# Token sums between the MLP's additions, and the first frequencies loaded between two halves of the row transforms

## The chip, the cores and the metric

The kernel runs on one core of one Trainium2 chip. The metric is device time in microseconds (us). Before the change, three runs gave a median of 3037.29 us, from 3034.9 to 3040.88. TensorE (PE) multiplies and transposes, VectorE (DVE) and ScalarE (ACT) empty PSUM and do elementwise work, GpSimd (POOL) does elementwise work in SBUF, and SyncE (SP) issues all the DMAs.

## The reference

The input is one image of 48 x 48 tokens with 768 channels, in float32. Two layers follow each other.

The first is a transformer block: layer norm, attention with 12 heads and relative positions over rows and columns, a projection, a residual, a second layer norm and an MLP:

```python
x = shortcut + out
xn2 = layernorm(x, ln2_g, ln2_b)
h = jax.nn.gelu(xn2 @ mlp_w1 + mlp_b1, approximate=False)      # 768 -> 3072
return x + (h @ mlp_w2 + mlp_b2)                               # 3072 -> 768
```

The second is a mixing in the frequencies of the image, with 8 blocks of 96 channels:

```python
xf = jnp.fft.rfft2(x, axes=(1, 2), norm='ortho')               # rows, then columns
o1 = relu(complex block product of xf with w1, plus b1)
o2 = softshrink(complex block product of o1 with w2, plus b2)
y = jnp.fft.irfft2(o2, s=(H, W), axes=(1, 2), norm='ortho')    # columns, then rows
return y + x
```

(The two middle lines stand for the four real products in the reference.)

## The kernel before, in words

Up to the MLP nothing changes: queries, keys and values, attention and the projection come first. The tokens, with the residual added, lie in SBUF as `x1`, 18 tiles of 128 tokens by 768 channels.

**The MLP** (lines 893 to 1068) takes the tokens in three passes `p` of 768. Each product of matrices is done in seven block products instead of eight, from sums and differences of blocks. For this, `xt` holds a pass's normalised tokens with channels on the partitions, in four blocks (lower and upper channels, first and second 384 tokens), and `xs` holds three sums of them. `sums_of_tokens` (line 163) makes these with four VectorE subtractions of 128 x 1152 numbers; they appear in the profile as L158, L159, L160 and L161. The last of the four overwrites one of the blocks of `xt`.

In a pass, `hidden` makes 256 of the 3072 hidden units, and there are twelve such steps. Between its three parts the additions `added(p, n - 1, i)` (line 975) of the step before are set, for `i` of 0 to 2. Each is seven products of 128 x 384 in four PSUM banks `o0` to `o3`, and VectorE adds each product to `x1` or to a sum `acc`, straight from PSUM (L995, L1001). So TensorE can be ahead of VectorE by about as many products as there are banks. In steps 4 to 9 of passes 0 and 1, `normalised` makes the normalised tokens (`hat2`, six buffers) for the next pass.

After the twelfth step comes the border: `turned` transposes the next pass's tokens on TensorE, ACT and VectorE write them to `xt` (L1045, L1049), `sums_of_tokens` is called, the three last additions of the old pass follow, and then `rows_forward(p)`. That multiplies the finished tokens with the Fourier matrix of the rows, first for the lower 384 channels (`k` of 0), then for the upper (`k` of 1). Each half has eight tiles in each pass: matmuls to `zp` in the same four banks, a copy to `zt` (four buffers; VectorE and ACT take turns, L77 and L75), and a store to the DRAM tensor `z1[k]` (L1026). The next pass's `hidden` comes after that.

**The spectral part** (lines 1070 to 1258) reads `z1` back in 14 units, seven for each half of the channels, of four frequencies each (the seventh has one). A unit is loaded as one tile `zi` (L1130, three buffers) and goes through four stages, one a round: `columns` (Fourier over columns, `fp`), `first` and `second` (the two block products, `lp` and `mp2`), and `back` (inverse over columns, `yp`; stored to `z2` at L1215). In one round four units are at work, each in another stage. `rows_back` is a generator for a group of 384 tokens and one half of the channels: a load of `zo` (L1222), then three steps of row transform (`rps`), addition of `x1`, and store. From round 11 on, its steps for the first half of the channels are set one by one between the stages; those of the second half follow at the end.

**What sets the order.** In the MLP and in the spectral part only TensorE's order is that of the program (`manual_schedule`). On the other engines and on SP's queue of DMAs, a planner chooses when the program is built: it goes by the order of the program, its own costs and what its costs say is ready. An engine and SP's queue then run in the order chosen, and an instruction that waits holds all behind it. A tile waits for the last use of the memory that it lies on. The pools of a closed part of the program give their memory to the next part, so such waits also run between parts.

Of the kernel before, what the change touches and what calls it, by code (L numbers as in the profile page):

```python
# [9 lines left out]
F32 = mybir.dt.float32  # L10
# [3 lines left out]
ALU = mybir.AluOpType  # L14
# [4 lines left out]
P = 128  # L19
HW = 48  # L20
T = HW * HW
NT = T // P
C = 768
# [6 lines left out]
G = 384  # L30
NB = 8
BS = C // NB
CH = C // 2
KW = HW // 2 + 1
# [10 lines left out]
def block_then_afno(  # L45
# [25 lines left out]
    nc = tc.nc  # L71
# [22 lines left out]
    z1 = [dram.tile([HW * 2 * KW, CH], F32, name=f"z1_{k}") for k in range(2)]  # L94
# [14 lines left out]
    xt = shared[:, : NC * TB].rearrange("p (c t) -> p c t", c=NC)  # L109
    xs = shared[:, NC * TB :].rearrange("p (k c t) -> p k c t", k=3, c=3)  # L110
# [46 lines left out]
    def right(eng, b11, b12, b21, b22, t):  # L157
        eng.tensor_tensor(t[0], b12, b11, ALU.subtract)  # L158
        eng.tensor_tensor(t[1], b22, t[0], ALU.subtract)  # L159
        eng.tensor_tensor(t[2], b21, t[1], ALU.subtract)  # L160
        eng.tensor_tensor(b12, b22, b12, ALU.subtract)  # L161

    def sums_of_tokens(xt, xs):
        lo, hi = xt[:, 0:3], xt[:, 3:6]
        right(
            nc.vector, lo[:, :, :G], lo[:, :, G:], hi[:, :, :G], hi[:, :, G:],
            [xs[:, i] for i in range(3)],
        )

    def parts_of_tokens(xt, xs, at=slice(None)):  # L170

# [13 lines left out]
    with ExitStack() as flag_scope:  # L185
# [11 lines left out]
        with ExitStack() as att:  # L197
# [314 lines left out]
            with tc.manual_schedule(engines={mybir.EngineType.PE, mybir.EngineType.SP}):  # L512
# [70 lines left out]
                for n, (pr, c, u) in enumerate(runs):  # L583
# [9 lines left out]
                    for i in range(RUN):  # L593
                        kt = RUN * u + i
                        p = exps[:, (RUN * n + i) % 18]
# [7 lines left out]
                    if pr < NC - 1:  # L603
                        if (c, u) in ((3, 1), (4, 0), (4, 1)):
                            i = 2 * (2 * (c - 3) + u - 1)
# [55 lines left out]
        with tc.tile_pool(name="ps_flag", bufs=1, space=PSUM) as psum, tc.tile_pool(  # L661
            name="ps_early", bufs=2, space=PSUM
# [29 lines left out]
        with tc.If(safe < 1):  # L692
            with ExitStack() as att:
                xnT = main.rearrange("p (c t) -> p c t", c=NC)
                with tc.tile_pool(name="g_ln1", bufs=3) as ln1, tc.tile_pool(
                    name="g_ps_ln1", bufs=2, space=PSUM
                ) as psum:
                    for g in range(T // G):
                        hats = []
# [179 lines left out]
        with tc.tile_pool(name="ps_proj", bufs=2, space=PSUM) as psum:  # L879
            hats = []  # L880
            for t in range(EARLY, NT):
# [8 lines left out]
                if n == 5:  # L890
                    sums_of_tokens(xt, xs)

    with ExitStack() as mlp:
        bias = mlp.enter_context(tc.tile_pool(name="mlp_const", bufs=1))
        b2 = bias.tile([P, C], F32, name="b2")
# [79 lines left out]
        def added(p, n, i):  # L975

            h, hs, v, vs = kept[p, n]
            bank = [psum.tile([P, CH], F32, name=f"o{k}") for k in range(4)]
            if n == 0:
                acc[i] = upool.tile([P, CH], F32, name=f"acc{i}", bufs=1)  # L980
            a11, a12, s3, a22 = (
                h[:, f, ds(k * G + i * P, P)] for f, k in ((0, 0), (1, 0), (0, 1), (1, 1))
            )
            s1, s2, s4 = (hs[:, k, ts(i, P)] for k in range(3))
            b11, t3, b21, b22 = (v[:, f, ts(k, CH)] for f in range(2) for k in range(2))
            t1, t2, t4 = (vs[:, k] for k in range(3))
            t = 2 * (p * 3) + i
            x11, x12, x21, x22 = (
                x1[:, t + 3 * j, ts(k, CH)] for j in range(2) for k in range(2)
            )  # L990

            def product(k, a, b, start, *into):
                nc.tensor.matmul(bank[k], a, b, start=start, stop=True, skip_group_check=not start)  # L993
                for dst in into:
                    nc.vector.tensor_tensor(dst, bank[k], dst, ALU.add)  # L995

            nc.tensor.matmul(bank[0], a11, b11, start=True, stop=True)  # L997
            if n == 0:
                nc.vector.tensor_copy(acc[i], bank[0])
            else:  # L1000
                nc.vector.tensor_tensor(acc[i], bank[0], acc[i], ALU.add)  # L1001
            product(1, s2, t2, True, acc[i])
            product(2, s3, t3, True, x22)
            product(3, s1, t1, True, x22)
            product(0, a12, b21, False, x11)
            product(2, a22, t4, False, x21)
            product(3, s4, b22, False, x12)
            if n == n_f - 1:
                nc.vector.tensor_tensor(x21, x21, acc[i], ALU.add)
                nc.gpsimd.tensor_tensor(x12, x12, acc[i], ALU.add)  # L1010
                nc.gpsimd.tensor_tensor(x22, x22, acc[i], ALU.add)

        def rows_forward(p):

            for k in range(2):
                for g in (2 * p, 2 * p + 1):
                    for a, parts in enumerate(((0,), (1, 2), (3, 4), (5,))):
                        zp = psum.tile([2 * 2 * KW, CH], F32, name="zp", tag=f"o{a}")
                        for b in parts:
                            nc.tensor.matmul(  # L1020
                                zp, rows_dft[:, b, :], x1[:, 3 * g + b // 2, ts(k, CH)],
                                start=(b == parts[0]), stop=(b == parts[-1]),
                            )
                        zt = upool.tile([2 * 2 * KW, CH], F32, name="zt", bufs=4)
                        balanced_copy(a, zt, zp)
                        nc.sync.dma_start(out=z1[k][ts(4 * g + a, 4 * KW), :], in_=zt)  # L1026

        hats = {}

        def normalised(p, i):  # L1030

            t = 6 * p + i
            hats[i] = hpool.tile([P, C], F32, name="hat2", bufs=6)
            normalise(upool, x1[:, t, :], hats[i])
            nc.gpsimd.tensor_tensor(x1[:, t, :], x1[:, t, :], b2, ALU.add)

        def turned():
            for j in range(2):
                for c in range(NC):
                    tp = psum.tile([P, G], F32, name="tp2", tag=f"h{c % 4}")  # L1040
                    for i in range(3):
                        nc.tensor.transpose(tp[:, ts(i, P)], hats[3 * j + i][:, ts(c, P)], ident)
                    dst = xt[:, c, ts(j, G)]
                    if c % 2:
                        nc.scalar.activation(  # L1045
                            dst, tp, AF.Identity, bias=col(V_LN2B + c), scale=col(V_LN2G + c)
                        )
                    else:
                        nc.vector.tensor_scalar(  # L1049
                            dst, tp, col(V_LN2G + c), col(V_LN2B + c), ALU.mult, ALU.add  # L1050
                        )
            sums_of_tokens(xt, xs)

        with tc.manual_schedule(engines={mybir.EngineType.PE}):
            for p in range(T // TB):
                for n in range(n_f):
                    work = hidden(p, n)
                    for i in range(3):
                        next(work)
                        if n:  # L1060
                            added(p, n - 1, i)
                    if p < 2 and 4 <= n < 10:
                        normalised(p + 1, n - 4)
                if p < 2:
                    turned()
                for i in range(3):
                    added(p, n_f - 1, i)
                rows_forward(p)

    with ExitStack() as sp:  # L1070
# [39 lines left out]
        nc.vector.tensor_scalar(a2i[:, :, 0, :], a2[:, :, 1, :], -1.0, None, ALU.mult)  # L1110
        nc.vector.tensor_copy(a2i[:, :, 1, :], a2[:, :, 0, :])

        z1_h = [z.rearrange("(r k) c -> r k c", k=KW) for z in z1]
        z2_h = [z.rearrange("(h t k) c -> h t k c", t=2, k=KW) for z in z2]
        NBH = NB // 2

        class Unit:
# [8 lines left out]
                self.zz = []  # L1126

            def load(self):
                self.zi = zin.tile([2 * HW, 4, CH], F32, name="zi", bufs=3)
                nc.sync.dma_start(  # L1130
                    out=self.zi[:, : self.nk, :],
                    in_=z1_h[self.half][:, self.k0 : self.k0 + self.nk, :],
                )

            def columns(self, i):

                if i == 0:
                    self.xf = mid.tile([BS, NBH, 2, 4, HW], F32, name="xf")
                if i >= self.nk:
                    return  # L1140
                fp = psum.tile([BS, NBH, 2, HW], F32, name="fp", tag="f")
                for b in range(NBH):
                    nc.tensor.matmul(  # L1143
                        fp[:, b].rearrange("p t h -> p (t h)"), self.zi[:, i, ts(b, BS)], cols,
                        start=True, stop=True,
                    )
                balanced_copy(i, self.xf[:, :, :, i, :], fp)
# [96 lines left out]
        with tc.manual_schedule(engines={mybir.EngineType.PE}):  # L1244
            first_half = pieces(ends[0])
            for r in range(len(units) + 3):
                if r < len(units):
                    units[r].load()
                for i in range(4):
                    for stage, lag in (("back", 3), ("second", 2), ("first", 1), ("columns", 0)):  # L1250
                        if 0 <= r - lag < len(units):
                            getattr(units[r - lag], stage)(i)
                    if r > len(units) // 2 + 3:
                        next(first_half, None)
            for _ in first_half:
                pass
            for _ in pieces(ends[1]):
                pass
# [128 lines left out]
```

## Time and profile before

| | us |
|---|---|
| median of three runs (lowest, highest) | 3037.29 (3034.9, 3040.88) |
| the profiled execution, its own time | 3041.24 |
| its span, from first to last instruction | 3039.4 |
| TensorE busy | 2947.5 |
| VectorE busy | 1784.6 |
| ScalarE busy | 869.5 |
| GpSimd busy | 569.2 |
| mean granted clock of TensorE | 0.99 |

In the profile a group of lines is named by its source line and engine, with the tile written, the tiles read, the shape and the count. A matmul in float32 is two instructions. A wait is put down to what ended it. The MLP lasts from about 1661 us to 2726 us of the span, with borders between the passes at about 1975 and 2335 us; the spectral part follows up to the end.

### The profile page before, as it was taken

To read this page: it belongs to the slowest core of one execution; us is meant where nothing else is said; L and a number is where in the kernel's file an instruction comes from. 1 tells how busy PE (TensorE), PEld (TensorE's weight loads), DVE (VectorE), ACT (ScalarE), POOL (GpSimd) and SP (SyncE) were. 2 spreads that over 40 slices of the span, in tenths; PEclk is the share of its full clock that TensorE was granted. 3 is DMA by queue.
4 is the path that set the end of the run, shared out by engine and by line. 5 is a ranking of instruction groups with operands and counts; after the bars stand their busy time and mean duration, and the time that the engine had idled before them with its cause. 6 is when DMAs were issued, how large, how long until landed. Compare 5 with 4: busy or idle time off the path is not lost. (4 is left out here: it accounts for less than half of the span.)

```text
span 3039.4 us, 40414 instructions
## 1 busy us (share of the span) xinstructions
PE 2947.5 (97%) x15495; PEld 1783.8 (59%) x15495; DVE 1784.6 (59%) x2582; ACT 869.5 (29%) x1346; POOL 569.2 (19%) x510
## 2 busy tenths in 40 slices
PE   6999999999999999999999999989999999989998
PEld 3555655655555565555555555555555555548885
DVE  4332327777777777777624766666666566653443
ACT  1010126565556565565401111121111111101110
POOL 2302110000000000000233332243223222211210
PEclk9999999999999999999999999999999999999999
DMA  3423276172552616344331111121111211131324
GB/s 110 144 80 115 97 158 123 29 134 56 87 114 50 135 32 132 64 81 74 130 116 46 52 63 63 52 64 63 62 53 52 74 62 52 52 94 55 90 70 151
DMA packets 204144, 253.37 MB, mean 83 GB/s; under 512 B 21698, under 2 KB 185762, under 8 KB 202406
## 3 DMA queue, kind: packets, MB, share of 16 engines
q1 hardware_dynamic: 203942, 250.69, 32.6%
q8 instruction: 125, 2.05, 0.3%
q14 instruction: 77, 0.63, 0.1%
HBM read 136.77 MB, written 50.14 MB: 61 GB/s over the span
## 5 line engine op out<-in xcount | busy, mean ns | idle before, releaser
L598 DVE TENSOR_TENSOR acc<-acc,main 128x768 f32<-128x768 f32 x576 | 551.9, 958 | 202.0 <-ACT main L541 145.3
L541 ACT ACTIVATE main<-sp 128x768 f32<-128x768 f32 x648 | 522.6, 812 | 155.4 <-PE sp L537 148.6
L537 PE MATMUL sp<-terms,select 64*128 64x384 f32 x1296 | 412.1, 629 | 0.0
L995 DVE TENSOR_TENSOR main<-o,main 128x384 f32<-128x384 f32 x540 | 298.7, 556 | 41.6 <-PE o L993 3.8
L933 PE MATMUL h<-shared,w 128*128 128x384 f32 x864 | 296.4, 486 | 0.8 <-issue 0.8
L531 PE MATMUL sp<-shared 64*128 64x384 f32 x1296 | 266.3, 488 | 2.8 <-DVE o L435 2.2
L531 PE MATMUL sp<-qT,kT 64*128 64x384 f32 x1296 | 266.5, 487 | 0.0
L424 PE MATMUL m<-main 128*128 128x384 f32 x756 | 250.1, 492 | 13.5 <-DVE o L435 8.9
L576 POOL TENSOR_TENSOR inverse<-inverse,rden 128x384 f32<-128x384 f32 x36 | 46.3, 1287 | 1028.9 <-DVE rden L573 961.6
L933 PEld LDWEIGHTS h<-shared,w 128*128 128x128 f32 x864 | 164.1, 190 | 115.7 <-issue 1.4
L933 PE MATMUL h<-shared,w1s 128*128 128x384 f32 x648 | 226.6, 486 | 0.0
L546 PE MATMUL op<-main,shared 128*64 128x384 f32 x1296 | 221.3, 488 | 0.0
L546 PE MATMUL op<-main,v 128*64 128x384 f32 x1296 | 219.9, 488 | 0.0
L424 PEld LDWEIGHTS m<-main 128*128 128x128 f32 x756 | 144.3, 192 | 117.0 <-issue 16.1
L939 ACT ACTIVATE hT<-c,vec 128x384 f32<-128x384 f32 x108 | 66.4, 615 | 464.9 <-DVE c L945 464.8
L945 DVE TENSOR_TENSOR c<-h,u 128x384 f32<-128x384 f32 x108 | 60.2, 557 | 212.3 <-PE h L933 212.3
L993 PE MATMUL o<-w,hT 128*128 128x384 f32 x432 | 175.5, 488 | 2.4 <-DVE mv L118 1.5
L993 PE MATMUL o<-w2s,hs 128*128 128x384 f32 x432 | 176.2, 490 | 1.0 <-DVE hs L153 1.0
L537 PEld LDWEIGHTS sp<-terms,select 64*128 64x128 f32 x1296 | 125.2, 186 | 83.8
L933 PEld LDWEIGHTS h<-shared,w1s 128*128 128x128 f32 x648 | 123.1, 190 | 85.9
L531 PEld LDWEIGHTS sp<-shared 64*128 64x128 f32 x1296 | 117.0, 186 | 60.8 <-issue 22.6
L546 PEld LDWEIGHTS op<-main,v 128*64 128x64 f32 x1296 | 89.9, 137 | 107.0 <-issue 107.0
(157 smaller groups left out, 3863.7 us busy)
## 6 DMA issues: line engine op xcount, KB each, us to landing
w<-in_mlp_w_dram SPq DMA_DIRECT2D x72, 768.0 KB
terms<-col_parts SPq DMA_DIRECT2D x432, 72.0 KB
terms<-row_hi SPq DMA_DIRECT2D x216, 72.0 KB
terms<-row_lo SPq DMA_DIRECT2D x216, 72.0 KB
main<-in_qkv_w_dram SPq DMA_DIRECT2D x36, 384.0 KB
z<-zt SPq DMA_DIRECT2D x48, 150.0 KB
z<-y SPq DMA_DIRECT2D x50, 144.0 KB
zo<-z SPq DMA_DIRECT2D x12, 600.0 KB
```

Of the source, the lines that this page charges most:

```text
L424: nc.tensor.matmul(bank, a[:, c, :], b[:, c, :], start=(first and c == 0), stop=(c == 2), skip_group_check=not first,)
L531: nc.tensor.matmul(sp[:, j, :G], kT[at, ts(kt, P)], qT[at, ts(c, G)], start=True, stop=False,)
L537: nc.tensor.matmul(sp[:, j, :G], select[at, a % 2], ready[pr, c][at, a // 2, b], start=False, stop=True,)
L541: nc.scalar.activation(p, sp[:, :, :G], AF.Exp, scale=HD**-0.5)
L546: nc.tensor.matmul(op[ts(j, 64)], v[:, kt0 + i, ts(j, 64)], ps[i][:, j, :], start=(kt0 + i == 0), stop=(kt0 + i == NT - 1),)
L576: nc.gpsimd.tensor_tensor(inverse, inverse, rden, ALU.add)
L598: nc.vector.tensor_tensor(acc, made[0] if kt == 1 else acc, p, ALU.add)
L933: nc.tensor.matmul(bank[i], a[:, c, :], b[:, c, :], start=(start and c == 0), stop=(c == 2), skip_group_check=not start,)
L939: nc.scalar.activation(h[:, i, ts(k, G)], src, AF.Gelu, bias=col(V_B1 + 2 * n + i))
L945: nc.vector.tensor_tensor(t, src, other, ALU.add)
L993: nc.tensor.matmul(bank[k], a, b, start=start, stop=True, skip_group_check=not start)
L995: nc.vector.tensor_tensor(dst, bank[k], dst, ALU.add)
```

## The change

It has four parts.

- `sums_of_tokens` takes a `piece`: 0, 1 and 2 are the first, the second, and the last two of the same four subtractions. For the sums of passes 1 and 2, `turned` no longer calls it, and one piece follows each of the three last additions. The sums of pass 0 are made as before, all at once, at the end of the projection.
- A pool `turn` is opened ahead of the MLP and stays open to the end. It has six buffers of 128 x 768, used by `hat2` and then by `zi`, and the four buffers of `zt`. These leave the MLP's pools, so that the pools' other tiles move to other addresses.
- `load_frequencies` loads four frequencies in two tiles of two. In the last pass it is called for the first two units after `rows_forward` has made the lower half (`k` of 0), so ahead of the upper half in the program. All other units load in this way too, at the place where they did.
- The steps of `rows_back` for the first half of the channels begin in round 12 instead of 11, so four of its steps follow after the loop.

```diff
-    def sums_of_tokens(xt, xs):
-        lo, hi = xt[:, 0:3], xt[:, 3:6]
-        right(
-            nc.vector, lo[:, :, :G], lo[:, :, G:], hi[:, :, :G], hi[:, :, G:],
-            [xs[:, i] for i in range(3)],
-        )
+    def sums_of_tokens(xt, xs, piece=None):
+
+        b11, b12, b21, b22 = (xt[:, ds(3 * i, 3), ts(j, G)] for i in range(2) for j in range(2))
+        t1, t2, t4 = (xs[:, i] for i in range(3))
+        steps = ((t1, b12, b11), (t2, b22, t1), (t4, b21, t2), (b12, b22, b12))
+        for i, (dst, a, b) in enumerate(steps):
+            if piece is None or piece == min(i, 2):
+                nc.vector.tensor_tensor(dst, a, b, ALU.subtract)
...
+    turn = ctx.enter_context(tc.tile_pool(name="turn", bufs=6))
+    first_loads = []
+
+    def load_frequencies(half, k0):
+
+        rows = z1[half].rearrange("(r k) c -> r k c", k=KW)
+        tiles = []
+        for k in range(k0, min(k0 + 4, KW), 2):
+            n = min(2, KW - k)
+            zi = turn.tile([P, C], F32, name="zi", tag="turn")
+            zi = zi[: 2 * HW].rearrange("p (k c) -> p k c", c=CH)
+            nc.sync.dma_start(out=zi[:, :n], in_=rows[:, k : k + n, :])
+            tiles.append(zi)
+        return tiles
...
-                        zt = upool.tile([2 * 2 * KW, CH], F32, name="zt", bufs=4)
+                        zt = turn.tile([2 * 2 * KW, CH], F32, name="zt", bufs=4)
                         balanced_copy(a, zt, zp)
                         nc.sync.dma_start(out=z1[k][ts(4 * g + a, 4 * KW), :], in_=zt)
+                if (p, k) == (2, 0):
+                    first_loads.extend(load_frequencies(0, k0) for k0 in (0, 4))
...
-            hats[i] = hpool.tile([P, C], F32, name="hat2", bufs=6)
+            hats[i] = turn.tile([P, C], F32, name="hat2", tag="turn")
...
-            sums_of_tokens(xt, xs)
...
                 for i in range(3):
                     added(p, n_f - 1, i)
+                    if p < 2:
+                        sums_of_tokens(xt, xs, i)
                 rows_forward(p)
...
-                self.zi = zin.tile([2 * HW, 4, CH], F32, name="zi", bufs=3)
-                nc.sync.dma_start(
-                    out=self.zi[:, : self.nk, :],
-                    in_=z1_h[self.half][:, self.k0 : self.k0 + self.nk, :],
-                )
+                self.zi = first_loads.pop(0) if first_loads else load_frequencies(self.half, self.k0)
...
-                        fp[:, b].rearrange("p t h -> p (t h)"), self.zi[:, i, ts(b, BS)], cols,
+                        fp[:, b].rearrange("p t h -> p (t h)"), self.zi[i // 2][:, i % 2, ts(b, BS)], cols,
...
-                    if r > len(units) // 2 + 3:
+                    if r > len(units) // 2 + 4:
                         next(first_half, None)
```

More of the change, by code (lines that the diff above doesn't have):

```diff
@@ L1111, in block_then_afno @@
         nc.vector.tensor_copy(a2i[:, :, 1, :], a2[:, :, 0, :])
-        z1_h = [z.rearrange("(r k) c -> r k c", k=KW) for z in z1]
         z2_h = [z.rearrange("(h t k) c -> h t k c", t=2, k=KW) for z in z2]
```

## The prediction

> **What bounds the kernel now.** I began with the page. It says that TensorE is the bound of nearly all of the run, so a change can only help where TensorE stands still or runs slowly:
>
> ```profile
> PE 2947.5 (97%) x15495; PEld 1783.8 (59%) x15495; DVE 1784.6 (59%) x2582; ACT 869.5 (29%) x1346; POOL 569.2 (19%) x510
> ```
>
> The span is 3039.4 us, so TensorE is idle for 91.9 us. The waits of TensorE alone (engine, operation, who ended the wait: total us, times, longest us) say where the change can reach:
>
> ```profile
> PE o L993 <- DVE main L995: 10.3, 5, 5.1
> PE fp L1143 <- DMA zi<-z: 7.5, 1, 7.5
> PE tp L1042 <- DVE shared L1049: 6.5, 3, 3.0
> PE rps L1230 <- DMA zo<-z: 6.2, 1, 6.2
> ```
>
> The first and third lie at the two borders between token passes, the second ahead of the spectral part, the fourth ahead of the last row transforms. The timeline at the first border (start us, us, what) shows the cause of the first:
>
> ```profile
> 1985.47 2.69 DVE L158 TENSOR_TENSOR shared<-shared 128x1152 f32<-128x1152 f32 x1
> 1988.08 0.54 DVE L1001 TENSOR_TENSOR acc<-o,acc 128x384 f32<-128x384 f32 x1
> 1988.55 2.49 DVE L159 TENSOR_TENSOR shared<-shared 128x1152 f32<-128x1152 f32 x1
> 1990.96 1.35 DVE L161 TENSOR_TENSOR shared<-shared 128x1152 f32<-128x1152 f32 x1
> 1992.23 1.34 DVE L160 TENSOR_TENSOR shared<-shared 128x1152 f32<-128x1152 f32 x1
> 1993.50 0.54 DVE L995 TENSOR_TENSOR acc<-o,acc 128x384 f32<-128x384 f32 x1
> ...
> 1994.65 1.62 PE L993 MATMUL o<-w2s,hT 128*128 128x384 f32 x2 [5.06 <-DVE main L995]
> ```
>
> VectorE makes the four sums of the next tokens (7.9 us) while `added` already waits for it to empty four PSUM banks. The pair of matmuls after the wait takes 1.62 us instead of 0.81: the clock has fallen. Busy time by stretch (us; PE, PEld, DVE, ACT, POOL, then granted clock, DMA share, GB/s) holds the two borders' additions, and the first and second stretch of the spectral part:
>
> ```profile
> 1985.00:2008.35 23.35, 16.45 (x45) 8.34 (x43) 23.01 (x39) 2.74 (x6) 13.41 (x10) 0.85 0.00 0
> 2344.20:2364.40 20.20, 16.40 (x44) 9.11 (x43) 17.10 (x27) 0.92 (x2) 5.66 (x6) 0.83 0.00 0
> 2733.40:2746.00 12.60, 12.04 (x59) 11.23 (x60) 2.07 (x4) 1.37 (x3) 0.00 (x0) 0.51 0.39 93
> 2746.00:2763.50 17.50, 17.50 (x136) 17.50 (x135) 8.20 (x18) 3.60 (x9) 3.62 (x4) 1.00 0.14 35
> ```
>
> At the first border VectorE is busy for 23.0 of 23.35 us: it is the bound there. At the second it is not full, and the 0.83 clock costs as well. The spectral part starts at half clock for 12.6 us. Its start and the last border in the timeline:
>
> ```profile
> 2727.15 11.94 SPq L1130 DMA_DIRECT2D zi<-z  x4
> 2733.36 5.40 PE L1143 MATMUL fp<-shared,zi 96*96 96x96 f32 x32 [7.49 <-DMA zi<-z]
> ...
> 2998.64 0.55 SPq L1215 DMA_DIRECT2D z<-y  x1
> ...
> 3001.99 0.31 SPq L1222 DMA_DIRECT2D zo<-z  x1
> ...
> 3008.32 4.00 PE L1230 MATMUL rps<-zo,shared 100*128 100x384 f32 x6 [6.18 <-DMA zo<-z]
> ```
>
> The first load of frequencies is issued 1.3 us after the last row transform, and its data are there 6.2 us later. At the end, the last `y` is stored at 2998.64, the load of rows that needs it goes out 3.35 us later, and again 6.3 us pass.
>
> [...] the same sum takes 2.69 us beside GpSimd's additions of `b2` at the first border, 1.34 to 1.37 us at the second. [...]
>
> **The change part by part.**
>
> *Sums between additions, passes 0 and 1.* The same four instructions, in three pieces behind the adds of each `added`. Adds back to back start every 0.47 us (2360.05, 2360.52, 2360.99), so 24 of them are 11.2 us against 13.5 us of matmuls (42 at 0.322). The first two pieces come before the last adds, the third (two sums) falls into `rows_forward`, 15.6 us long, where VectorE works for only 8.2 and 5.5 us. Second border: 11.2 + 2 x 1.27 = 13.7 us, level with the 13.5; four banks absorb about 2 us of lag. I take 14.7 us against 20.2 now: **5.5 us**. Half of that is the clock that no longer falls. First border: the planner fills VectorE with the normalisation for pass 2 (3.9 us inside the stretch), and GpSimd slows the sums. 11.2 + 0.8 for a slowed add + 2.5 to 5.2 + 3.9 = 18.4 to 21.1 us from 1985.5, against 23.35 us: 2.3 to 5 us, more if the hats move out. I take **4.5 us**. The 3.0 us wait of the transposes (L1049 behind `left` of the hidden units) stays. What the third piece now delays is the first two copies of `zp`, by 2.5 us; TensorE returns to that bank after six matmul pairs, 3.9 us. Without that cover it would cost 2.5 us a border. The next hidden unit needs the last sum 15 us later.
>
> *First loads between the halves.* Four DMAs (units 0 and 4, two frequencies each) go to SP ahead of the second half's eight stores. They wait for the first half's last store, issued at about 2719.0; by the 3.35 us above they go out near 2722, with 4 x 0.32 us of issue. The first unit's 576 KB took 6.2 us, so it is there at about 2728.4 instead of 2733.36. Behind these instructions wait the second half's stores, for `zt` has four buffers: the copies of its last four tiles, and behind these on ACT and VectorE the copies of `xf`, can be held to about 2729. So TensorE idles for some 2.5 us, not 7.49: 5 us. [...] the half clock from 2733.4 to 2746 (6 us of loss) should mostly go; I count 4. **9 us**, between 0 (loads issued after all stores) and 13. Here too the old `zi` lay over `rows_dft` and waited for its last matmul; the new buffers are the hats', free since 2344.
>
> *Two loads a unit.* 12 more SP issues (26 loads for 14, the last unit of a half has one frequency) at 0.32 us, 3.8 us in all, on a queue that mostly waits; each round of the spectral part lasts 18 us and three units are still held. Zero; with no cover 0.3 us a unit.
>
> *Row transforms of the first half one round later.* One generator (12 matmuls, 3.9 us) leaves round 11, where columns, first, second and back keep TensorE full without it, and goes after the loop. The last `y` is stored 3.9 us earlier, its load goes out at about 2998.1 and is there at 3004.4; TensorE has 7.7 us of row transforms to do from 2994.2 to 3002. Idle 2.4 us instead of 6.18. The 2 us of half clock after it (32 matmuls in 12.38 us, not 10.3) may go too, but stores of 0.6 MB more share the DMA with the load, about 2.5 us at 217 GB/s. **4 us**, between -0.7 (SP issues the load behind the stores) and 6.
>
> *Moved buffers.* `hat2` and `zt` change addresses, and `b2` and `rows_dft` no longer lie on the projection's weights, whose last matmul held their load on SP for 49.9 us. What stood behind it was not late: TensorE begins the first hidden unit with 0.8 us idle. Zero, at most 1.5 us either way.
>
> Sum: 5.5 + 4.5 + 9 + 4 = 23 us. The profiled execution took 3041.24 us, so 3018.2; it lies 4 us above the median of the runs shown, 3037.29, and that becomes **3014.3 us**.
>
> **Rivals.** *The loads come no earlier*: SP issues them behind the second half's stores, or the stores' 1.2 MB slow them, and the half clock stays. For it: SP's order is the planner's, and both streams share one queue. Against: the buffers and the first half's data are ready 7 us before. The 9 us go, 3023. *VectorE stays the bound at the borders and the tail gains nothing*: hats fill the gaps, GpSimd slows the sums, only the third piece is gained (2.7 us each), SP's order eats the tail: 5.4 + 9 = 14.4, 3023. For it: 23.01 of 23.35 us busy; against: 17.10 of 20.20 at the second border. *The gains all turn into the next wait*: about 3033. *Slower*: the four loads hold SP, with the second half's stores behind them; `zt` runs out, ACT and VectorE stop at its copies, and TensorE at PSUM. The place is 2719 to 2733; each us that SP is held beyond 2725 moves the first spectral matmul by one. It outweighs the other 14 us once the first `lp` comes after 2753 (now 2739.3), SP held some 25 us: 3045. Against: the only thing waited for is a store that takes some 3 us.
>
> **How the numbers follow.** Forecast 0.60 (own range 3007 to 3021), loads no earlier 0.17, VectorE and tail 0.14, all given back 0.05, slower 0.04. Within 0.2% (6.1 us) is about what cannot be told from no change. Faster 0.91, same 0.05, slower 0.04. The range, 3004 to 3028, takes in the first three cases and the upper ends of the parts.
>
> **What would show it.** No wait of TensorE over 2 us in `added` at either border, clock above 0.95 there; SP's loads of `zi` before 2723 on today's scale and the wait of `fp` under 3 us; the stretch after it at clock near 1; the last wait for `zo` near 2.4 us. Wrong if VectorE's order puts hats ahead of the adds, or SP holds the second half's stores so long that `fp` waits over 5 us.

## The result, and the profile after

The changed kernel takes 3019.55 us in the median (3018.21 to 3021.65), against 3039.09 for the kernel before beside it: 0.9936 of it, 95% interval 0.9919 to 0.9953, or 19.5 us less. The forecast was 23 us less. Two later sets of runs of the same kernel gave 0.9958 (0.9946 to 0.9971) and 0.9942 (0.9927 to 0.9958), so the gain is better called 13 to 20 us.

The profiled execution took 3021.65 us, its span is 3019.8 us. TensorE's busy time is nearly what it was (2947.5 us before); what went is mostly idle time, 75 us where it was 92:

```profile
PE 2944.7 (98%) x15495; PEld 1780.9 (59%) x15495; DVE 1783.6 (59%) x2582; ACT 868.8 (29%) x1346; POOL 572.5 (19%) x510
```

The waits of TensorE that answer to the four shown of before (engine, operation, who ended the wait: total us, times, longest us; lines have moved, L1011 is the product of an addition, L1062 a transpose):

```profile
PE rps L1246 <- DMA zo<-z: 8.4, 4, 3.2
PE tp L1062 <- DVE shared L1069: 6.5, 3, 3.0
PE fp L1159 <- ACT zt L75: 3.8, 1, 3.8
PE o L1011 <- DVE main L1013: 3.3, 4, 1.2
```

The wait in the additions fell from 10.3 us to 3.3 and is never over 1.2 us. The transposes' wait is unchanged. `fp` waits 3.8 us instead of 7.5, for another reason: a copy to `zt` ends it, not the load. The last row transforms wait 8.4 us instead of 6.2, in four pieces instead of one.

At the first border, the timeline (start us, us, what) has a sum right behind one addition, and no wait of 5 us any more:

```profile
1982.78 2.21 DVE L170 TENSOR_TENSOR shared<-shared 128x1152 f32<-128x1152 f32 x1
1984.92 0.54 DVE L1013 TENSOR_TENSOR acc<-o,acc 128x384 f32<-128x384 f32 x1
1986.07 0.88 PE L1011 MATMUL o<-w2s,hT 128*128 128x384 f32 x2 [1.22 <-DVE main L1013]
```

The other three sums start at 1987.47, 1994.35 and 1998.45, the last one at the end of the additions. Busy time by stretch (us; PE, PEld, DVE, ACT, POOL, granted clock, DMA share, GB/s), for the two borders' additions and the first stretch of the spectral part:

```profile
1981.46:1998.70 17.24, 15.09 (x44) 7.38 (x43) 16.95 (x28) 0.87 (x2) 10.41 (x8) 1.00 0.00 0
2334.90:2350.80 15.90, 14.97 (x43) 7.70 (x43) 15.69 (x26) 0.67 (x1) 5.96 (x6) 0.98 0.00 0
2714.04:2726.70 12.66, 12.10 (x91) 11.93 (x92) 3.47 (x8) 2.56 (x6) 0.00 (x0) 0.87 0.42 126
```

The additions take 17.24 and 15.90 us instead of 23.35 and 20.20, at full clock or nearly. The spectral part starts at 0.87 instead of 0.51. At the first border VectorE does 28 instructions there instead of 39: the planner moved the normalisation for pass 2 out of the stretch. VectorE is still busy nearly throughout, but the adds come when TensorE needs them.

Ahead of the spectral part the timeline shows the four early loads go out at 2705.56 (2721.2 on the scale of before, 15.66 us more), and what stands behind them:

```profile
2705.56 1.71 SPq L907 DMA_DIRECT2D zi<-z  x4
2707.31 1.96 SPq L1044 DMA_DIRECT2D z<-zt  x4
...
2713.51 0.48 ACT L75 COPY zt<-zp 100x384 f32<-100x384 f32 x1 [4.67 <-DMA z<-zt]
...
2714.04 4.56 PE L1159 MATMUL fp<-shared,zi 96*96 96x96 f32 x32 [3.83 <-ACT zt L75]
```

The stores issued at 2707.31 have the loads' 1.2 MB ahead of them. Their `zt` buffers stay taken, ACT waits 4.67 us for a buffer (VectorE, for the copy before, 5.37 us, up to 2712.95), and `fp` waits for the last of those copies.

At the end, each later load of rows stands in SP's queue behind three stores of output that wait for their tiles:

```profile
2978.53 0.35 SPq L1238 DMA_DIRECT2D zo<-z  x1
2979.39 7.93 SPq L1250 DMA_DIRECT2D out_dram<-yt  x3
2980.91 11.26 PE L1246 MATMUL rps<-zo,shared 100*128 100x384 f32 x24 [2.14 <-DMA zo<-z]
2987.41 0.32 SPq L1238 DMA_DIRECT2D zo<-z  x1
...
3000.74 9.67 PE L1246 MATMUL rps<-zo,shared 100*128 100x384 f32 x24 [3.19 <-DMA zo<-z]
```

The first wait is 2.14 us, near the 2.4 us of the forecast. The next load goes out 8.9 us after the one before it, and TensorE catches up with it: 1.28, 3.19 and then 1.80 us more.

### The profile page after: what moved, and what is told of

Same layout as the page of the kernel before. It is cut to its first block, busy times and chain, and to the rows that moved or that the text cites. A ratio compares the mean times of both kernels' runs of the same rounds, so it can differ in the third digit from the quotient of the medians.

```text
span 3019.8 us, 40443 instructions
## 1 busy us (share of the span) xinstructions
PE 2944.7 (98%) x15495; PEld 1780.9 (59%) x15495; DVE 1783.6 (59%) x2582; ACT 868.8 (29%) x1346; POOL 572.5 (19%) x510
## 5 line engine op out<-in xcount | busy, mean ns | idle before, releaser
L1011 PE MATMUL o<-w,hT 128*128 128x384 f32 x432 | 174.9, 487 | 1.6 <-DVE mv L118 1.6
L1011 PE MATMUL o<-w2s,hs 128*128 128x384 f32 x432 | 174.9, 487 | 1.0 <-DVE hs L153 1.0
```

## The experiments

**How the parts are read.** Comparing two profiles needs care here. The stretch up to the first product of the attention scores, which no kernel changes, took between 436.5 and 446.1 us in the fourteen profiles; before had the 446.1 and after 440.7, so 5.4 of the 19.6 us between these two profiles are not the change. The table therefore takes the stretches that the change touches, from every profile: both borders' additions together; the third border, from the first row transform of pass 2 to the first `yp`; and the tail, from there to the end. In brackets is half of the time for which the clock was at half in that stretch, from the trace's clock records. At half clock a pair of 128 x 384 matmuls took 1.62 us, at full clock 0.81 (before, at 1994.65 and 1998.44). So that half is the most that it can cost: while TensorE stands still, half clock takes nothing from it.

| kernel | additions | third border | tail |
|---|---|---|---|
| before | 43.5 (6.8) | 53.3 (8.5) | 275.9 (3.5) |
| after | 33.1 (0.3) | 45.7 (1.7) | 279.5 (5.9) |
| after, second set | 33.9 (0.8) | 50.6 (6.8) | 274.6 (1.7) |
| after, third set | 33.1 (0.4) | 48.9 (5.1) | 275.6 (3.9) |
| after, round 11 | 33.8 (0.5) | 48.6 (5.1) | 276.0 (5.8) |
| before, round 12 alone | 42.4 (5.4) | 52.3 (6.8) | 275.1 (1.9) |
| before, sums alone | 33.1 (0.3) | 49.5 (3.4) | 276.7 (3.4) |
| after, sums whole again | 44.1 (7.2) | 49.0 (5.1) | 277.2 (5.8) |
| buffers and tiles alone | 44.2 (7.3) | 46.8 (5.1) | 276.8 (3.8) |
| after, no early call | 34.0 (0.9) | 41.6 (0.0) | 275.7 (1.9) |
| the same, again | 33.7 (0.7) | 41.5 (0.0) | 276.4 (2.4) |
| after, eight `zt` | 32.9 (0.0) | 41.2 (0.0) | 275.4 (3.8) |
| no early call, loads two ahead | 33.1 (0.0) | 42.2 (0.0) | 282.1 (6.8) |
| no early call, queue mended | 34.0 (0.9) | 44.9 (3.4) | 272.2 (3.9) |

In the first four expectations, "the prediction's step" is a step as forecast, and "the reading of the two traces" is a first comparison of the profiles of before and after: additions worth 10.4 us, loads 7.7, the tail a loss of 3.8.

**Is the tail a loss?** Two kernels: after with the first half's row transforms from round 11 again, and before with round 12 alone.

```diff
-                    if r > len(units) // 2 + 4:
+                    if r > len(units) // 2 + 3:
```

> The changed kernel with one part undone: the row transforms of the first half begin in round 11 again. The prediction's step (the later start is worth 4 us): 4 us slower than the changed kernel, 3023.5. The reading of the two traces (the later start costs 3.8 us, because SP then issues the last loads of rows behind the stores): 3.8 us faster, 3015.8, with one wait of TensorE for these loads of about 6 us in place of four.

> The kernel before with this part alone: the row transforms begin in round 12. The prediction's step: 4 us faster than before, 3035. The reading of the traces: 3.8 us slower, 3043, and SP's loads of rows for the second half one at a time between the stores.

The first gave 3025.62 us, ratio 0.9958 (0.9945 to 0.9971); after lies between 0.9936 and 0.9958 in its three sets, so this tells nothing finer than that the difference is below some 6 us. The second is clearer: 3039.2 against 3040.33 us, ratio 1.0000 (0.9987 to 1.0013). Round 12 alone shows no gain; the interval reaches 4 us either way, so a gain of 4 us lies at its very edge, and the tail in the profile is 275.1 us against 275.9. Its timeline shows where the forecast gain went:

```profile
2994.50 9.67 PE L1230 MATMUL rps<-zo,shared 100*128 100x384 f32 x24 [1.93 <-DMA zo<-z]
3006.20 4.11 PE L1230 MATMUL rps<-zo,shared 100*128 100x384 f32 x12 [2.02 <-DMA zo<-z]
...
3016.49 4.11 PE L1230 MATMUL rps<-zo,shared 100*128 100x384 f32 x12 [1.86 <-DMA zo<-z]
```

One wait of 6.2 us has become five that sum to 6.8. In before, SP had issued the next two loads soon after the first (3001.99), with one store between, and ahead of stores that wait:

```profile
3003.16 1.05 SPq L1222 DMA_DIRECT2D zo<-z  x2
3011.84 2.11 SPq L1234 DMA_DIRECT2D out_dram<-yt  x2
```

With round 12 each of these loads stands behind three such stores, as in after. The reading of the two traces was wrong too: the 3.8 us lost in the profile of after were partly half clock (at most 5.9 us there, 1.7 and 3.9 in the other two).

**Are the sums worth ten?** After with the sums at once in `turned` again, and, in a later set, before with the pieces alone.

```diff
                 if p < 2:
                     turned()
+                    sums_of_tokens(xt, xs)
                 for i in range(3):
                     added(p, n_f - 1, i)
-                    if p < 2:
-                        sums_of_tokens(xt, xs, i)
```

> The changed kernel with the four sums made at once ahead of the last additions again. The prediction (5.5 and 4.5 us) : 10 us slower than the changed kernel, 3029.5. The reading of the traces (6.1 and 4.3 us in the two stretches of additions): 10.4 us slower. The rival that VectorE stays the bound (2.7 us a border): 5.4 us slower, 3025.

> Before with the sums in three pieces between the additions and nothing else. Theory 'the borders, as forecast' (two gaps of 5 us close, half of the gain is the clock): 10 us below before, ratio 0.9967. Theory 'sums are the whole change' (undoing them gave back 18 us): 17 to 19 us below before, ratio 0.994, and then the other parts sum to nothing. In the profile both: the additions take 16 to 18 us at both borders instead of 23.4 and 20.2; the border ahead of the spectral part as before, with TensorE waiting some 7 us for the first load.

Without the pieces nearly all is given back: 3037.88 us, ratio 0.9995 (0.9985 to 1.0005). That looked as if the sums were the whole change. The pieces alone gave 3029.28 against 3039.21 us, ratio 0.9969 (0.9955 to 0.9983), 10 us, as the prediction had them. Its waits show the additions' wait gone and that of `fp` as before:

```profile
PE fp L1146 <- DMA zi<-z: 7.5, 1, 7.5
...
PE o L995 <- DVE main L997: 3.4, 5, 1.2
```

Of the 10.4 us in the table's first column, some 6 are waiting and 4 are half clock. In before, the clock is at half for 6.83 us in each border's additions (from 1991.41 and from 2349.81 us), and TensorE is busy for 3.59 and 5.20 us of them; half of that is 4.4 us, and with the pieces 0.3 are left. What remains, 6.3 us, fits the waits, which fell by 6.9 us. The other parts of the change then had to sum to about 3 us in this set (the kernel after was 12.6 us below before in it), and the question was why the loads, whose stretch is shorter, bring so little.

**Does the early call make the third border shorter?** After without the call, the tiles of two frequencies and the buffers kept:

```diff
-                if (p, k) == (2, 0):
-                    first_loads.extend(load_frequencies(0, k0) for k0 in (0, 4))
```

> The changed kernel without the early call: the first two units are loaded after all row transforms, still in two tiles each. The prediction: 9 us slower than the changed kernel, 3028.5. The reading of the traces (3.7 us less waiting, 4.1 us less half clock): 7.7 us slower, 3027. If the gain there came from the moved buffers and not from the call, no difference.

It gave 3018.4 us, ratio 0.9937 (0.9919 to 0.9956): not slower than after, which had 0.9936 to 0.9958. So the call wasn't the cause, and the border had become shorter still, 41.6 us. To find the cause, all but the buffers and the tiles was taken out of after: no call, sums at once, round 11.

> The kernel after without the pieces of the sums, without the early call of the loads, and with the row transforms from round 11: what is left is the pool of its own for hats, zt and the loads, and the loads in two tiles. Theory 'the early call makes the gain' (as forecast): within 2 us of before. Theory 'the gain is the address' (the old load lay on the Fourier matrix of the rows and had to wait for its last matmul; free buffers let the queue's order take the loads among the stores by itself): first load before 2712 on the scale of after, the wait for it gone, 7 to 11 us below before at this border (ratio 0.9964 to 0.9977).

> The kernel after, unchanged, run again beside the parts, so that sums of parts are made on one chip. Both theories: 18 to 21 us below before (ratio 0.993 to 0.995). What a second profile of the same program shows differently (stages whose code is the same, the granted clock) is the noise of a single profile.

The buffers and tiles alone gave 3030.6 against 3039.21 us, ratio 0.9975 (0.9966 to 0.9984), 8.6 us. In the same set after had 3026.63 us, ratio 0.9958. So the gain that the prediction put on the call comes without it, from the buffers and tiles. In before, the memory of the first `zi` overlaps that of the Fourier matrix of the rows, so it could not be loaded before that matrix's last matmul (the program's memory plan says so; the trace names no such wait). All 16 stores of the last pass stand ahead of the first load in SP's queue:

```profile
2711.89 14.79 SPq L1026 DMA_DIRECT2D z<-zt  x16
```

With buffers that are free, the planner sets the loads among the stores without any call. SP's queue in the kernel with the buffers and tiles alone, and the first matmuls behind it, which no longer wait for a load:

```profile
2710.23 9.03 SPq L1044 DMA_DIRECT2D z<-zt  x10
2719.56 0.31 SPq L907 DMA_DIRECT2D zi<-z  x1
2720.31 1.57 SPq L1044 DMA_DIRECT2D z<-zt  x3
...
2725.74 4.59 PE L1156 MATMUL fp<-shared,zi 96*96 96x96 f32 x32 [1.54 <-ACT zt L75]
```

This set doesn't part the buffers from the halving of the tiles: that it is the addresses is argued from the order of SP's queue, and no run here shows it.

**Does the call cost, and through `zt`?** After, after without the call, and after with the call and eight `zt` buffers, in one set:

```diff
-                        zt = turn.tile([2 * 2 * KW, CH], F32, name="zt", bufs=4)
+                        zt = turn.tile([2 * 2 * KW, CH], F32, name="zt", bufs=8)
```

> The kernel after, unchanged, beside the same kernel without the early call. Theory 'the early call adds nothing, or costs' (the loads' bytes lie ahead of the second half's stores, and the first matmuls wait for the last of these tiles): 2 to 6 us above the kernel without the call. Theory 'the call is worth 9 us' (as forecast): 5 us or more below it. In the profile again a wait of 3.8 to 4.4 us for the last copy to zt.

> The kernel after without the early call, again, on the same chip as the one with it. Theory 'adds nothing, or costs': ratio to before 0.993 to 0.995, with the wait ahead of the spectral part at 1 to 1.5 us. Theory 'worth 9 us': ratio 0.998.

> The kernel after, early call kept, with eight zt buffers instead of four, so that the copies of the second half never wait for a store. Theory 'four buffers run out behind the loads': the wait of the first fp falls from 3.8 to 4.4 us to under 1 us, and the time is 3 to 7 us below the kernel after in the same call (the wait, and the half clock that sometimes follows it). Theory 'the loads themselves are late': the wait stays over 3 us, now ended by the load.

After: 3026.17 us, ratio 0.9942 (0.9927 to 0.9958). Without the call: 3019.24 us, 0.9924 (0.9909 to 0.994). With the call and eight buffers: 3017.98 us, 0.9911 (0.9897 to 0.9926). The first matmuls of the spectral part in these three, in this order:

```profile
2721.05 5.44 PE L1159 MATMUL fp<-shared,zi 96*96 96x96 f32 x32 [4.13 <-ACT zt L75]
```

```profile
2715.49 3.32 PE L1157 MATMUL fp<-shared,zi 96*96 96x96 f32 x32 [0.86 <-ACT zt L75]
```

```profile
2715.78 3.31 PE L1159 MATMUL fp<-shared,zi 96*96 96x96 f32 x32 [0.57 <-ACT zt L75]
```

With eight buffers SP issues the same four loads together, still ahead of six stores, and `fp` waits 0.57 us:

```profile
2710.48 1.71 SPq L907 DMA_DIRECT2D zi<-z  x4
2712.24 4.86 SPq L1044 DMA_DIRECT2D z<-zt  x6
```

So the wait of about 4 us in after is the four `zt` buffers running out behind the loads; that is shown. Its cost against eight buffers is 8.2 us in the medians, and the intervals just part. The profiles say why it is more than the wait: in the third set the third border is some 3 us shorter even without its half clock (48.9 less 4.8 us, against 41.2), and half clock behind the wait cost 1.7, 6.2 and 4.8 us in the three profiles of after (half of TensorE's busy time in it) and nothing in that with eight. The call against no call is 6.9 us the wrong way, with intervals that overlap a little. Across the sets it is less clear, since the kernel without the call had 0.9937 in its first set and after 0.9936 in its own; the third border is clearer, 45.7 to 50.6 us in the three profiles of after against 41.5 to 44.9 in the four without the call. The call with eight buffers and no call with four are the same within their intervals; no call with eight wasn't tried.

**Can SP's queue be mended at the end?** First, loads put two groups ahead of their row transforms in the program, with four `zo` buffers and without the early call:

```diff
+            late = ends[1]
+            for gen in late[:2]:
+                next(gen)
             for _ in first_half:
                 pass
-            for _ in pieces(ends[1]):
-                pass
+            for g, gen in enumerate(late):
+                for nxt in late[g + 2 : g + 3]:
+                    next(nxt)
+                for _ in gen:
+                    pass
```

> The kernel after without the early call, with four buffers for the rows read back, and each of their loads at the end put two groups ahead of its row transforms in the program. Theory 'the queue's order eats the tail' (each late load stands behind three stores that wait for their tiles): the four waits of the last row transforms for their loads, 8.4 us in the profile of after, fall to one of 2 to 4 us; 4 to 6 us below the same kernel without this (3018.4), ratio to before 0.991 to 0.9925. Theory 'the loads are slow by themselves' (they share the DMA engines with the stores): waits and time stay, 0.9937.

3022.97 us, ratio 0.9946 (0.9934 to 0.9959): nothing gained over 0.9937 without it. The waits of TensorE hold a single, longer one:

```profile
PE rps L1244 <- DMA zo<-z: 11.6, 1, 11.6
```

The planner had put the load of the last group of the first half third in the queue, behind two loads of the second half, though TensorE needs it first. So neither theory was tested by that. In the next kernel this load is issued two rounds earlier, the rest as here:

```diff
+                if r == len(units) + 1:
+                    next(ends[0][-1])
```

> The kernel after without the early call, with four zo buffers, the load of the last group of the first half issued two rounds earlier, and the loads of the second half one group ahead of their row transforms in SP's queue. Against the earlier try (two ahead, whose 11.6 us wait was the first half's last load standing third in the queue): theory 'the queue's order eats the tail': all waits for zo together under 4 us, 3 to 5 us below the kernel without the early call, ratio to before 0.992. Theory 'the loads are slow by themselves': one wait of 4 us or more for the second half's first load stays, and the time is that of the kernel without the early call.

3013.01 us (3012.32 to 3017.73), ratio 0.9905 (0.989 to 0.9919): 6.2 us below the kernel without the call in the same set, with intervals that overlap, so the time alone doesn't settle it. SP's queue and TensorE's row transforms:

```profile
2979.33 0.36 SPq L1236 DMA_DIRECT2D zo<-z  x1
2980.24 2.91 SPq L1248 DMA_DIRECT2D out_dram<-yt  x3
2983.25 0.37 SPq L1236 DMA_DIRECT2D zo<-z  x1
2984.37 15.18 PE L1244 MATMUL rps<-zo,shared 100*128 100x384 f32 x36 [2.18 <-DMA zo<-z]
2999.82 4.14 PE L1244 MATMUL rps<-zo,shared 100*128 100x384 f32 x12 [0.26 <-DVE yt L1247]
```

Each load goes out one group ahead. The waits for `zo` fall from 7.1 us in the kernel without the call to one of 2.18 us, and the tail is 272.2 us, the shortest of all; without the brackets 268.3 against 274.0. The kernel tried before this one differs from it by the place of one load alone, has the same four `zo` buffers, and gained nothing. So it is the queue's order that had eaten the tail. This kernel has the lowest median of those tried, about 29 us below before; eight `zt` buffers with it weren't tried.

## Why the prediction was right, and where not

The total came out near the forecast partly by luck. Of the 23 us, 13 were put on two steps that brought nothing or cost time, and 8.6 us came from a part that had been counted as zero.

*Sums between additions*: right. 10 us were forecast, 10 measured alone. The first border gave more than its 4.5 (23.35 to 17.24 us), because the hats did move out, which the prediction had left as an extra. The second gave less than 5.5 (20.20 to 15.90). The third piece's delay stayed covered: the row transforms behind it take 15.48 us in before and 15.49 in after.

*First loads between the halves*, 9 us: this is the step that failed. The prediction saw that the old `zi` waited for the last matmul on `rows_dft` and that the new buffers were free, and it saw the stores queue behind the loads. It put the gain on the call all the same, and counted the buffers at zero. The runs have it the other way round: 8.6 us for the buffers and tiles alone, and some 7 us back for the call with its four `zt` in the one set that compares them. The forecast wait of 2.5 us was 3.8 to 4.4. The way in which the call costs is that of the prediction's rival *Slower*, `zt` running out behind the loads, only smaller. That 4 us of half clock would go with a shorter wait was the author's estimate, and the runs don't bear it out: waits of only 1.34 us (queue mended) and 1.54 us (buffers and tiles alone) were followed by 6.83 and 10.24 us at half clock. Nor was the clock soon back in before: the prediction's own line with 0.51 granted is 12.60 us long, and TensorE is busy for 12.04 of them.

*Moved buffers*, zero, at most 1.5 us either way: wrong by that same 8.6 us, in which the halved tiles are included.

*Row transforms one round later*, 4 us: wrong; nothing was seen. The step costed the first load alone (2.4 us, 2.14 and 1.93 measured) and not the five behind it, which SP now holds behind stores. Its lower end, -0.7 us, named SP's order, but for the first load. The 3.35 us that the prediction read as a wait for the store of `y` show this order already: two stores of output, which wait for VectorE, stand between that store and the load, from 3000.18 to 3001.81 us, and the load goes out right behind them.

*Two loads a unit*, zero: the stretch from the first to the last `yp` is 234.02 us in before and also with buffers and tiles alone. Right.

So 10 for the sums, 8.6 for the buffers, some 7 lost by the call and nothing at the tail make about 12; measured were 13 to 20. Parts of such size don't add up better than a few us here. Of the signs that were to show it, the clock and the waits of the additions and the time of the loads were right; the wait of `fp` under 3 us, the clock near 1 behind it (0.87) and the single wait at the end were not.

## What to carry to other kernels

When a load comes late, look first at whose memory its buffer lies on; with a free buffer the planner may move the load by itself. A call that forces it showed no gain on top of that here, and with four `zt` it pushed stores back. When a transfer is moved ahead of stores in a queue, count the buffers of those stores, for they stay taken longer: here the copies that needed them waited 4.67 and 5.37 us. When a wait at a chain of loads is shortened, follow the second and third load through the queue as well, not only the first.

## What the runs showed of the hardware

The size of the clock's losses was not expected. In the clock records of before and after, nineteen stretches at half clock end within the execution: thirteen are 3.41 us long, five 6.83 and one 17.07. So 3.41 us of it cost at most 1.7 us, half of that. Two stretches of before at its slowest place, the second right behind the first (columns as above, the clock is the third from the end):

```profile
2728.70:2732.11 3.41, 0.00 (x0) 0.00 (x0) 0.00 (x0) 0.00 (x0) 0.00 (x0) 0.50 0.99 243
2732.11:2745.77 13.66, 11.85 (x56) 11.09 (x57) 2.07 (x4) 1.37 (x3) 0.00 (x0) 0.50 0.45 107
```

After the idle 3.41 us the clock stays at half for 13.66 us more, though TensorE is busy for 11.85 of them; in the 3.41 us after these it is 1.00. In these two traces every stretch at half clock starts a whole number of times 3.413 us after the first one of its execution, for instance 6, 442, 558 and 858 times in before and 6, 423, 662 and 852 times in after. A wait had no fixed price in these runs: behind the wait of about 4 us ahead of `fp`, TensorE lost 1.7, 6.2 and 4.8 us to the clock in three executions of the kernel after (half of its busy time at half clock), and behind the 7.5 us wait 5.9 in before and 1.9 with the sums alone; behind a wait of 1.34 us 3.1 were lost in the kernel with the mended queue, and behind waits of 0.57 to 1.02 us nothing in four others. Over 28 runs of before, the time goes with the mean granted clock (correlation -0.88), 2.8 us for each thousandth, and reaches from 3029.86 to 3045.78 us; in the two other sets, of 27 and 11 runs, the correlation is -0.83 and -0.45. So a saving of a few us by one wait is only seen in a median over many runs, and closing a wait of 4 us was worth more than its 4 us here (8.2 us in the medians, with intervals that just part).
